# A graph layer with top-p attention: queries split by other engines in the opening, late keys and their load moved between the steps

## The chip, the cores and the metric

The kernel runs on one core of one Trainium2 chip. The core has five engines with a queue each: TensorE (PE: matmuls and transposes into PSUM; its weight loads are shown apart as PEld), VectorE (DVE), ScalarE (ACT), GpSimd (POOL) and SyncE (SP), which here only issues DMAs. Each engine works off its own queue in order and waits on semaphores for the others. The metric is the device time of one execution in microseconds (us).

## The reference

3327 nodes with 256 features each, a sparse weighted adjacency (about 0.12% of the entries beside the diagonal), two steps. Cut to what matters:

```python
def top_p_attention(X, W1, W2, W3):
    q = X @ W1.T @ W2.T                      # 64 wide
    k = X @ W3.T
    probs = softmax(q @ k.T)
    # per row: sort, keep the largest entries until their sum reaches 0.9, drop the rest
    A = probs * mask
    return A / A.sum(-1)

h = relu(layernorm(x))
R = adj + I;  R = R / R.sum(-1)
Xf = Xa = h;  Z = 0
for n in range(2):
    A  = top_p_attention(Xa, W1, W2, W3)
    Xf = R @ Xf
    Xa = A @ Xa
    Z  = Z + Xf @ U1[n].T + Xa @ U2[n].T
out = x + layernorm(h + Z) * ln_g + ln_b
```

## The kernel before, in words

Rows are handled in NT = 26 tiles of 128 nodes (P = 128); NP = 3328 columns. Two fp32r halves stand for one fp32 number: a value is rounded (high part) and the rest is kept beside it (low part), so that the logits of a tile are two accumulating matmuls per 512 columns. `keys` (128 x 3328) holds the rounded keys in rows 0 to 63 and the rest in rows 64 to 127. The queries lie split in DRAM as `qx` and whole as `asks` on the chip.

**Opening** (L1060 to L1130). A loop over q treats the tiles in 13 pairs k, as a pipeline written in program text: at q = k the statistics of the layer norm (DVE, POOL: `rn`), at q = k + 1 the Relu (ACT) and PE's transposes into `pt`, at q = k + 2 ACT's copy of them (`xw` in the rows) and the products for keys and queries into the PSUM tile `pk`, at q = k + 3 the copies out of it, at q = k + 4 the split of keys and queries and the stores. `pk` and `pt` share two PSUM buffers. At q = k + 3 ACT writes the rounded keys (L1064, `keys`), DVE the raw keys and queries (L1065, `kq`) and, for pairs that enter the moments, a copy `krs` (L1067). At q = k + 4 DVE subtracts the rounded keys from the raw ones (L1104), POOL casts the queries (L1106, `qs`) and subtracts (L1107), and SP stores `kq` into `asks` (two DMAs, L1109) and `qs` into `qx` (L1110). `kq` and `qs` are drawn from one set of four buffers with the tag s1. For the first three tiles `qs` is also sent on as the queries `qT` of the first logits (`fetch`, L550).

In the same loop, at q = 5 to 14, `listed` (L862) reduces the adjacency of one tile, in halves of 832 KB, to lists of its nonzero blocks: SP loads a half one ahead (L869, into `wide` and `e`), DVE reduces it (L879, `fm`). After the loop come the moments of the keys, three tiles' `project` (L562 to L577, DVE, ACT and POOL) and the first tile's guess. The order of the opening is not written out: the planner of the tile framework orders each queue by the program's order and by what its cost model holds to be ready, and it makes an instruction wait for a buffer until its last reader is done. Products for the diffusion (`products`, L1027: PE L1039, copies L1045, stores L1046 and L1047) start in the opening and run on in the first tiles.

**Steps** (L1176 to L1280). From `begin` on, each engine's order is the order of the text (L1283 to L1287; SP's until step 1 starts). For step 0 and 1 and i = -1 to 27, seven parts k = 0 to 6 run what the strings of PLAN, BEGIN, OPEN and LAST name by letters: w is a tile's logits and exponentials (`weights`, four chunks of 832 columns, L634 and L636), d its settling on DVE (L756 to L794), s the sparse diffusion (L955, L1157, and the store L1160 of `vx`), e the end of a tile of step 0 (`first_end`, L963: PE L968, ACT L969 and L971, POOL L972, the store `sx`, and then `prep`).

`prep` (L497) makes the keys and queries of step 1 from a finished tile of step 0. For tiles below SPOOLED = 22 the columns of `keys` are still in use, so the rounded and the low part go to `kx` in DRAM; for tiles 22 to 25 the keys are written in place (ACT L514, DVE L522), and POOL splits the queries (L523, L524). The stores are collected in a list and issued on SP by `stored` (L553): at part k = 4 of each i, and from i = 23 on also at the end of each i. At i = 24 SP issues the load of the 22 spooled tiles from `kx` into `keys` in three DMAs (L1233): tiles 0 to 6, 7 to 12 and 13 to 21. They wait for the stores that they read. The first three chunks of step 1's first tiles run from i = 24 on, the fourth in step 1.

Of the kernel before, what the change touches and what calls it, by code (L numbers as in the profile page):

```python
# [9 lines left out]
F32 = mybir.dt.float32  # L10
F32R = mybir.dt.float32r
# [4 lines left out]
ALU = mybir.AluOpType  # L16
# [3 lines left out]
P = 128  # L20
# [3 lines left out]
NT = (N + P - 1) // P  # L24
# [301 lines left out]
HALF = NT // 2  # L326
# [21 lines left out]
def guess_graph_layer(ctx, tc, x, adj, w1t, w2t, w3t, u1t, u2t, ln_g, ln_b, out, flag):  # L348
# [148 lines left out]
    def prep(xT, t):  # L497
        pk = ps_t.tile([P, 4, P], F32, tag="pt", name="pk")
        for c in range(ND):
            PE.matmul(pk[:, 0, :], wk[:, c, :], xT[:, c, :], start=c == 0, stop=c == ND - 1)  # L500
        if t in COUNTED:
            for c in range(ND):
                PE.matmul(pk[:, 1, :DA], xT[:, c, :], wk[:, c, :DA], start=c == 0, stop=c == ND - 1)
        kr = krs[:, t // 2 % 2, :]
        if t in COUNTED:
            S.copy(kr[:, :DA], pk[:, 1, :DA])
        kq = tpool.tile([P, P], F32, tag="kq", name="kq", bufs=2)
        hi = tpool.tile([P, P], F32R, tag="hi", name="hi", bufs=2)
        lo = tpool.tile([P, P], F32R, tag="lo", name="lo", bufs=2)
        at = slice(t * P, (t + 1) * P)  # L510
        if t < SPOOLED:
            S.copy(hi, pk[:, 0, :])
        else:
            S.copy(keys[low, at], pk[low, 0, :])  # L514
        S.copy(kq, pk[:, 0, :])
        yield
        if t < SPOOLED:
            G.tensor_tensor(lo, kq, hi.bitcast(F32), ALU.subtract)
            stores.append((kx[low, at], hi[low]))
            stores.append((kx[high, at], lo[low]))  # L520
        else:
            V.tensor_tensor(keys[high, at], kq[low], keys[low, at].bitcast(F32), ALU.subtract)  # L522
            G.tensor_copy(hi[high], kq[high])  # L523
            G.tensor_tensor(lo[high], kq[high], hi[high].bitcast(F32), ALU.subtract)  # L524
        stores.append((qx[high, at], hi[high]))
        stores.append((qx[low, at], lo[high]))
        stores.append((query_of(t), kq[high]))
        if t not in COUNTED:
            return
        pg = ps_t.tile([P, 4, P], F32, tag="pt", name="pg")  # L530
        PE.matmul(pg[:DA, 0, : DA + 1], kr[:, :DA], kr, start=True, stop=True)
        gt = small.tile([DA, DA + 1], F32, tag="gt", name="gt", bufs=2)
        S.copy(gt, pg[:DA, 0, : DA + 1])
        G.tensor_tensor(gsum, gsum, gt, ALU.add)
# [525 lines left out]
    for q in range(HALF + 5):  # L1060
        if 0 <= q - 3 < HALF:
            k, pk = q - 3, made.pop(q - 3)
            raw[k] = kq = row.tile([P, 2, P], F32, tag="s1", name="kq", bufs=4)
            S.copy(keys[low, 2 * k * P : (2 * k + 2) * P], pk[low, :2, :].rearrange("p t r -> p (t r)"))  # L1064
            V.tensor_copy(kq, pk[:, :2, :])  # L1065
            if 2 * k in COUNTED:
                V.tensor_copy(krs[:, k % 2, :DA], pk[:, 2, :DA])  # L1067
        if q < HALF:
            mv = small.tile([P, 2, 2], F32, tag="mv2", name="mv2", bufs=4)
            rn = small.tile([P, 2, 2], F32, tag="rn2", name="rn2", bufs=3)  # L1070
            for h in range(2):
                st = small.tile([P, 6], F32, tag="bn", name="st")
                V.bn_stats(st, x0[:, 2 * q + h, :])
                V.bn_aggr(mv[:, h, :], st)
            G.tensor_scalar(rn[:, 0, :], mv[:, :, 1], LN_EPS, None, ALU.add)
            G.tensor_tensor(rn[:, 0, :], rn[:, 0, :], half[:, 0::3], ALU.pow)
            G.tensor_tensor(rn[:, 1, :], mv[:, :, 0], rn[:, 0, :], ALU.mult)
            G.tensor_scalar(rn[:, 1, :], rn[:, 1, :], -1.0, None, ALU.mult)
            scaled[q] = rn
        if 5 <= q < 15:  # L1080
            run(lister, 1)
        if 0 <= q - 2 < HALF:
            k, pt = q - 2, turned.pop(q - 2)
            S.copy(hT[:, 2 * k : 2 * k + 2].rearrange("p t c r -> p (t c) r"), pt)
            pk = ps_t.tile([P, 4, P], F32, tag="pt", name="pk")
            for c in range(ND):
                PE.matmul(pk[:, :2, :], wk[:, c, :], hT[:, 2 * k : 2 * k + 2, c, :], start=c == 0, stop=c == ND - 1)
            if 2 * k in COUNTED:
                for c in range(ND):
                    PE.matmul(pk[:, 2, :DA], hT[:, 2 * k, c, :], wk[:, c, :DA], start=c == 0, stop=c == ND - 1)  # L1090
            made[k] = pk
        if 0 <= q - 1 < HALF:
            k, rn = q - 1, scaled.pop(q - 1)
            pt = ps_t.tile([P, 4, P], F32, tag="pt", name="pt")
            for h in range(2):
                t = 2 * k + h
                S.activation(x0[:, t, :], x0[:, t, :], AF.Relu, bias=rn[:, 1, h : h + 1], scale=rn[:, 0, h : h + 1])
                for c in range(ND):
                    PE.transpose(pt[:, 2 * h + c, :], x0[:, t, c * P : (c + 1) * P], ident)
            turned[k] = pt  # L1100
        if 0 <= q - 4 < HALF:
            k, kq = q - 4, raw.pop(q - 4)
            at = keys[:, 2 * k * P : (2 * k + 2) * P]
            V.tensor_tensor(at[high], kq[low].rearrange("p t r -> p (t r)"), at[low].bitcast(F32), ALU.subtract)  # L1104
            qs = row.tile([P, 2, P], F32R, tag="s1", name="qs", bufs=4)
            G.tensor_copy(qs[high], kq[high])  # L1106
            G.tensor_tensor(qs[low], kq[high], qs[high].bitcast(F32), ALU.subtract)  # L1107
            for h in range(2):
                nc.sync.dma_start(query_of(2 * k + h), kq[high, h, :])  # L1109
            nc.sync.dma_start(qx[:, 2 * k * P : (2 * k + 2) * P], qs.bitcast(F32).rearrange("p t r -> p (t r)"))  # L1110
            for h in range(2):
                if 2 * k + h < 3:
                    fetch(0, 2 * k + h, qs[:, h, :])
        if 0 <= q - 4 < HALF and 2 * (q - 4) in COUNTED:
            k = q - 4
            kr = krs[:, k % 2, :]
            PE.matmul(pgram[:DA, : DA + 1], kr[:, :DA], kr, start=2 * k == COUNTED[0], stop=2 * k == COUNTED[-1])
        if q == 6:
            run(begun[0], 1)
        if q in (8, 11, 14):  # L1120
            run(begun[0], 1)
        if q in (9, 12):
            run(begun[q // 3 - 2], 1)
        if q == 5:
            for n in range(2):
                nc.sync.dma_start(u1[:, :, n], u1t[n].rearrange("(c p) e -> p c e", p=P))
# [68 lines left out]
    for step in range(2):  # L1195
        sums = Sums(step, live, xw if step else x0, AHEAD[step])

        for i in range(-1, NT + 2):
# [30 lines left out]

                work["w"] = itertools.islice(begun[i - NT + 2], CUT - 1)  # L1230
            if step == 0 and i == NT - 2:
                for a, b in ((0, 7), (7, 13), (13, SPOOLED)):
                    nc.sync.dma_start(keys[:, a * P : b * P].bitcast(F32), kx[:, a * P : b * P])  # L1233
            if step == 0 and i >= NT - 3 and i < NT:
                fetch(1, i - NT + 3)
# [3 lines left out]
            if step == 0 and i == 0:  # L1239
                work["w"] = begun[2]  # L1240
            for k in range(PARTS):
                if step == 0 and k == 4:
                    stored()
                g = PARTS * (i - 1) + k - LATE[step]
                summing = valid(g // PARTS)
                if step and valid((g + AHEAD[1]) // PARTS):
                    sums.turn(g + (k == 2), min(i, NT - 1))
                for c in ({**OPEN, **LAST} if step else BEGIN).get(i, PLAN[step])[k]:
                    at = len(trace)
                    next(work[c], None)  # L1250
                    if c == "g" and not step and len(trace) > at:
                        gate = next(n for n in reversed(trace[:at]) if n.engine == S.engine)
                        issue = next(n for n in trace[at:] if n.engine == G.engine)
                        tc.add_manual_dep(issue, gate.name, BEHIND, reason="one by one")
                if summing and not step:
                    sums.turn(g, min(i, NT - 1))
                for n in BLOCKS[step].get(k, (0,)) if summing else ():
                    ended = sums.sum(g + n)
                    if ended and step == 0:
                        live["r", ended[0]] = ended[1]  # L1260
                    elif ended:
                        work["f"] = finish(ended[0], live.pop(("f", ended[0])), *ended[1])
# [5 lines left out]
                next(fetching)  # L1268
            for c in ("lcnwqsepb" if i > -1 else "cnwqsepb") if step else "ocmwqseph" + "b" * (i > 0):
                run(work[c])  # L1270
            if step == 0 and i >= NT - 3:
                stored()
            if step == 0 and i == NT:
                moments(1, gsum)
# [53 lines left out]
```

## Time and profile before

| | |
|---|---|
| median of 3 runs | 1392.1 us (1389.31 to 1393.02) |
| the profiled execution | 1390.78 us, its span 1389.0 us |
| instructions | 22547 |
| PE busy | 1239.2 us, 89% |
| PEld busy | 1030.9 us, 74% |
| DVE busy | 1196.2 us, 86% |
| ACT busy | 1068.8 us, 77% |
| POOL busy | 1036.2 us, 75% |
| opening and first tiles | to about 190 us |
| steady part of step 0 | about 190 to 620 us |
| between the steps | about 620 to 830 us |

A row of the view in order of time gives start, duration, engine, line, operation, output <- input and shapes; what stands in brackets is how long the engine was idle before it, and what ended that. SPq is SP's queue: its rows are the issue of a DMA, not the transfer. In the list of groups the number after the bar is busy us and mean ns, and after the second bar the idle time before the group with its releasers. A row of waits reads: engine, line, what it waited for, total us, times, longest us.

### The profile page before, as it was taken

The page shows a single profiled execution, that of the slowest core. Times are in us where ns is not written, and L with a number is a line of the kernel's source. Part 1 is how long each engine was busy: PE and PEld are TensorE (multiplying, and loading weights), DVE is VectorE, ACT ScalarE, POOL GpSimd, SP SyncE. Part 2 cuts the span into 40 slices and gives each one's busy share as a digit, 9 for nine tenths or more (in the row PEclk, how much of TensorE's full clock was granted, in tenths as well). Part 3 has the DMA queues.
Part 4 walks back from the last instruction along what each step waited for, and adds up shares of the span by engine and source line. Part 5 has one row for each costly group of instructions (what it writes and reads, how often), then busy time and mean ns, then how long its engine had stood idle before and what let it go on. Part 6 is the DMA issues. An engine that isn't in the chain of part 4 may idle for free.

```text
span 1389.0 us, 22547 instructions
## 1 busy us (share of the span) xinstructions
PE 1239.2 (89%) x6340; PEld 1030.9 (74%) x6340; DVE 1196.2 (86%) x3652; ACT 1068.8 (77%) x2226; POOL 1036.2 (75%) x1460
## 2 busy tenths in 40 slices
PE   5759899999999999999879849999999999999985
PEld 4524688888887888888768647878878887787874
DVE  5748789999999999999874489899998999999994
ACT  5365687878788887878754589898998989999851
POOL 6322588888888888887865477888888888888832
PEclk9989999999999999999999979999999999999998
DMA  5844555555555555555544222313223132231200
GB/s 182 268 155 130 148 147 157 151 163 154 166 147 171 145 165 149 152 165 150 151 125 125 71 64 59 99 54 99 71 79 94 56 97 70 81 95 50 89 23 22
DMA packets 123191, 164.59 MB, mean 118 GB/s; under 512 B 21137, under 2 KB 89232, under 8 KB 123056
## 3 DMA queue, kind: packets, MB, share of 16 engines
q1 hardware_dynamic: 105520, 120.14, 27.9%
q0 software_dynamic: 16640, 42.69, 12.0%
q8 instruction: 53, 0.87, 0.3%
q14 instruction: 82, 0.67, 0.2%
q10 hardware_dynamic: 896, 0.21, 0.1%
HBM read 128.74 MB, written 32.12 MB: 116 GB/s over the span
## 4 chain that ended last, share of the span: by engine, by line
DVE 51%; PE 15%; ACT 14%; POOL 9%; issue 4%; DMA 3%; SPq 1%; DVEq 0%; POOLq 0%; ACTq 0%
DVE cand L761 9%; DVE w L756 8%; ACT ja L660 8%; DVE e L790 8%; PE pa L849 6%; DVE fm L879 5%; DVE cand L770 4%; DVE bb L768 4%; PE pl L634 2%; PE pz L1039 2%; ACT e L636 2%; PE pt L836 2%; POOL xg L947 2%; POOL g L739 2%; PE pr L955 1%
## 5 line engine op out<-in xcount | busy, mean ns | idle before, releaser
L660 ACT ACTIVATE ja<-e,g 128x3328 uint8<-128x3328 f32 x106 | 325.9, 3074 | 0.1
L849 PE MATMUL pa<-x,eT 128*128 128x256 f32 x1352 | 322.0, 379 | 0.0
L849 PE MATMUL pa<-xw,eT 128*128 128x256 f32 x1352 | 318.1, 380 | 3.0 <-DVE s L979 3.0
L849 PEld LDWEIGHTS pa<-xw,eT 128*128 128x128 f32 x1352 | 251.3, 190 | 36.1 <-DVE s L979 4.9
L849 PEld LDWEIGHTS pa<-x,eT 128*128 128x128 f32 x1352 | 242.8, 190 | 25.5
L761 DVE MAX8 cand<-w 128x8 f32<-128x168 f32 (+1 forms) x1040 | 253.3, 317 | 0.0
L838 ACT COPY eT<-pt 128x512 f32<-128x512 f32 (+1 forms) x364 | 199.4, 555 | 61.1 <-PE pt L836 61.0
L947 POOL DMA_INDIRECT xg<-bx,index x130 | 189.7, 1460 | 51.5 <-issue 21.9
L634 PE MATMUL pl<-keys,qT 128*128 128x512 f32 (+1 forms) x832 | 200.4, 377 | 26.3 <-ACT e L636 13.7
L836 PE MATMUL pt<-ident,e 128*128 128x128 f32 x1144 | 176.5, 277 | 48.5 <-DVE e L790 34.5
L926 POOL DMA_INDIRECT ac<-in_adj,index x130 | 163.3, 1256 | 67.6 <-ACT e L1045 18.8
L836 PEld LDWEIGHTS pt<-ident,e 128*128 128x128 f32 x1144 | 141.5, 145 | 89.2 <-issue 50.9
L636 ACT ACTIVATE e<-pl 128x832 f32<-128x832 f32 (+1 forms) x176 | 150.6, 862 | 44.9 <-PE pl L634 41.9
L634 PEld LDWEIGHTS pl<-keys,qT 128*128 128x128 f32 x832 | 145.2, 195 | 52.0 <-ACT e L636 15.9
L947 POOL DMA_INDIRECT xg<-vx,index x130 | 150.5, 1158 | 34.1 <-issue 32.8
L756 DVE SCALAR_TENSOR_TENSOR w<-e,g 128x3328 f32<-128x3328 f32 x44 | 164.3, 3734 | 4.2 <-ACT g L741 4.1
L790 DVE SCALAR_TENSOR_TENSOR e<-e,rec 128x3328 f32<-128x3328 f32 x40 | 148.3, 3708 | 0.6
L955 PE MATMUL pr<-xg,ac 128*128 128x257 f32 (+1 forms) x520 | 139.1, 392 | 10.1 <-DVE s L1157 8.4
L955 PEld LDWEIGHTS pr<-xg,ac 128*128 128x128 f32 x520 | 95.4, 195 | 21.8 <-DVE s L1157 8.8
L768 DVE MAX8 bb<-cand 128x8 f32<-128x160 f32 x286 | 92.6, 324 | 6.4
L879 DVE TENSOR_REDUCE fm<-at 128x4 f32<-128x512 f32 (+1 forms) x133 | 84.3, 634 | 5.5 <-DMA at<-in_adj 5.5
L703 POOL TENSOR_SCALAR g<-g,law 128x1 f32<-128x1 f32 x23 | 65.6, 2850 | 10.9 <-ACT g L702 10.1
(260 smaller groups left out, 2018.4 us busy)
## 6 DMA issues: line engine op xcount, KB each, us to landing
at<-in_adj SPq DMA_DIRECT2D x114, 256.0 KB
cx<-ac SPq DMA_DIRECT2D x26, 384.0 KB
ac<-cx SPq DMA_DIRECT2D x26, 384.0 KB
wide<-in_adj SPq DMA_DIRECT2D x8, 832.0 KB
qT<-qx SPq DMA_DIRECT2D x196, 32.0 KB
e<-in_adj SPq DMA_DIRECT2D x6, 832.0 KB
own<-bx SPq DMA_DIRECT2D x26, 128.5 KB
x<-in_x SPq DMA_DIRECT2D x13, 256.0 KB
```

Source lines behind the costliest of these rows:

```text
L634: PE.matmul(pl[:, a:b], qT[:, k, :], keys[:, c + a : c + b], start=k == 0, stop=k == 1)
L636: S.activation(e[:, c : c + w], pl[:, :w], AF.Exp, accum_out=za[:, n : n + 1])
L660: S.activation(ja, e, f, bias=guess, scale=sign, accum_out=total)
L756: V.scalar_tensor_tensor(w, e, col(16), e, ALU.is_lt, ALU.mult, accum_out=d2)
L761: V.max(cand[:, 8 * s : 8 * s + 8], w[:, s * SEG : min(NP, (s + 1) * SEG)])
L790: V.scalar_tensor_tensor(e, e, at(1), e, ALU.is_ge, ALU.mult, accum_out=ra)
L836: PE.transpose(pt[:, j, :], e[:, (j0 + j) * P : (j0 + j + 1) * P], ident)
L838: S.copy(eT[:, :w, :], pt[:, :w, :])
L849: PE.matmul(self.pa, eT[:, c - 4 * k, :], self.xa[:, c, :], start=c == 0, stop=c == NT - 1)
L926: G.indirect_dma_start(out=ac[:, k, :], out_offset=None, in_=rows, in_offset=bass.IndirectOffsetOnAxis(ap=index[:, t, k : k + 1], axis=0), ...
L947: G.indirect_dma_start(out=xg[:, k, :w], out_offset=None, in_=rows, in_offset=bass.IndirectOffsetOnAxis(ap=index[:, t, k : k + 1], axis=0))
L955: PE.matmul(pr[:, :w], ac[:, k, :], own if k == KT - 1 else xg[:, k, :w], start=k == 0, stop=k == KT - 1)
```

## The change

Two places. In the opening, ACT copies and casts the queries out of PSUM at q = k + 3 (`qs[high]`), beside its copy of the keys, and DVE subtracts at q = k + 4; POOL has no part in it. `qs` has buffers of its own, those of the tags own and xa (two each, taken in turn), and `kq` keeps the four of s1 alone. The stores of `kq` and `qs` and the sending on to `qT` move from q = k + 4 to q = k + 5.

Between the steps, the low part of the keys of tiles 22 to 24 is subtracted by POOL instead of DVE (tile 25 stays with DVE). The load of the spooled keys is issued in two places: tiles 0 to 12 where all three DMAs were, and tiles 13 to 21 at part k = 2 of the same i, behind the stores of tile 21, which are issued there too (at k = 2 and not at k = 4, and not at the end of the i before). The stores at the end of an i are left at i = 27 only.

```diff
@@ prep
-            V.tensor_tensor(keys[high, at], kq[low], keys[low, at].bitcast(F32), ALU.subtract)
+            (V if t == NT - 1 else G).tensor_tensor(keys[high, at], kq[low], keys[low, at].bitcast(F32), ALU.subtract)
@@ opening, for q in range(HALF + 5)
         if 0 <= q - 3 < HALF:
             k, pk = q - 3, made.pop(q - 3)
-            raw[k] = kq = row.tile([P, 2, P], F32, tag="s1", name="kq", bufs=4)
+            kq = row.tile([P, 2, P], F32, tag="s1", name="kq", bufs=4)
+            qs = row.tile([P, 2, P], F32R, tag=("own", "xa")[k % 2], name="qs", bufs=2)
             S.copy(keys[low, 2 * k * P : (2 * k + 2) * P], pk[low, :2, :].rearrange("p t r -> p (t r)"))
+            S.copy(qs[high], pk[high, :2, :])
             V.tensor_copy(kq, pk[:, :2, :])
+            raw[k] = kq, qs
...
         if 0 <= q - 4 < HALF:
-            k, kq = q - 4, raw.pop(q - 4)
+            k, (kq, qs) = q - 4, raw[q - 4]
             at = keys[:, 2 * k * P : (2 * k + 2) * P]
             V.tensor_tensor(at[high], kq[low].rearrange("p t r -> p (t r)"), at[low].bitcast(F32), ALU.subtract)
-            qs = row.tile([P, 2, P], F32R, tag="s1", name="qs", bufs=4)
-            G.tensor_copy(qs[high], kq[high])
-            G.tensor_tensor(qs[low], kq[high], qs[high].bitcast(F32), ALU.subtract)
+            V.tensor_tensor(qs[low], kq[high], qs[high].bitcast(F32), ALU.subtract)
+        if 0 <= q - 5 < HALF:
+            k, (kq, qs) = q - 5, raw.pop(q - 5)
             for h in range(2):
                 nc.sync.dma_start(query_of(2 * k + h), kq[high, h, :])
             nc.sync.dma_start(qx[:, 2 * k * P : (2 * k + 2) * P], qs.bitcast(F32).rearrange("p t r -> p (t r)"))
...
@@ steps
             if step == 0 and i == NT - 2:
-                for a, b in ((0, 7), (7, 13), (13, SPOOLED)):
+                for a, b in ((0, 7), (7, 13)):
                     nc.sync.dma_start(keys[:, a * P : b * P].bitcast(F32), kx[:, a * P : b * P])
...
             for k in range(PARTS):
-                if step == 0 and k == 4:
+                if step == 0 and k == (2 if i == NT - 2 else 4):
                     stored()
+                    if i == NT - 2:
+                        nc.sync.dma_start(keys[:, 13 * P : SPOOLED * P].bitcast(F32), kx[:, 13 * P : SPOOLED * P])
...
-            if step == 0 and i >= NT - 3:
+            if step == 0 and i == NT + 1:
                 stored()
```

## The prediction

> **What bounds the kernel now.** I read the page first, then a table of stretches, and inside the two stretches that the change touches the groups, the waits and the instructions in order of time. A count before a name in brackets, such as (x57), is a number of instructions.
>
> ```profile
> core 0: us, PE busy (x) PEld busy (x) DVE busy (x) ACT busy (x) POOL busy (x), PEclk, DMA share, GB/s
> 27.14:69.39 42.25, 32.09 (x160) 23.02 (x160) 28.62 (x79) 17.83 (x38) 16.97 (x39) 0.96 0.75 234
> ...
> 190.00:620.00 430.00, 418.02 (x2244) 355.12 (x2244) 412.39 (x1290) 356.56 (x845) 366.10 (x441) 1.00 0.56 157
> ...
> 702.00:778.00 76.00, 67.68 (x342) 55.99 (x340) 37.25 (x123) 30.61 (x77) 42.57 (x59) 0.96 0.40 116
> ```
>
> In the long steady stretch of step 0 PE and DVE are both 96 to 97% busy; the change does not touch it, so whatever is won or lost ahead of it should move it as a whole. The two stretches that are touched have slack: in 42.25 us of the opening the busiest engine works 32.09, and between the steps DVE works 37 of 76.
>
> In the opening the third and the thirteenth copy of raw keys and queries (kq) start at 27.14 and 69.39: ten stages, 4.2 us each. What sets that pace is a loop through a shared buffer. From the instructions in order of time:
>
> ```profile
> 27.14 0.42 DVE L1065 COPY kq<-pk 128x256 f32<-128x256 f32 x1 [1.43 <-ACT keys L1064]
> ...
> 54.76 1.11 SPq L1109 DMA_DIRECT2D asks<-kq  x2
> ...
> 56.50 0.40 POOL L1106 CAST qs<-kq 64x256 fp32r<-64x256 f32 x1 [0.90 <-DMA asks<-kq]
> ...
> 56.98 0.72 POOL L1107 TENSOR_TENSOR qs<-kq,qs 64x256 fp32r<-64x256 f32 x1
> ...
> 57.70 0.41 DVE L1065 COPY kq<-pk 128x256 f32<-128x256 f32 x1
> ...
> 69.39 0.41 DVE L1065 COPY kq<-pk 128x256 f32<-128x256 f32 x1
> ```
>
> kq is copied (53.9 in the stage shown), SP stores it, POOL waits until that store has landed before it may write the split (qs) into a buffer of the same four, and the next kq starts at 57.70, as POOL ends (56.98 + 0.72). The waits, as us in total, times and longest, of POOL and DVE up to 150 us and of SP up to 110 us:
>
> ```profile
> POOL qs L1106 <- DMA asks<-kq: 15.7, 7, 5.4
> ...
> DVE fm L879 <- DMA e<-in_adj: 16.8, 4, 11.5
> ```
>
> ```profile
> SPq L1110 <- POOL qs L1107: 19.7, 10, 4.7
> ```
>
> SP stands 19.7 us behind POOL's split, and the loads of adj, which DVE's list reductions (fm) want, are queued behind it.
>
> Between the steps PE stops once:
>
> ```profile
> 701.84 0.38 PE L490 MATMUL pt<-ident,xa 128*128 128x128 f32 x2
> 709.84 3.14 PE L634 MATMUL pl<-keys,qT 128*128 128x512 f32 x8 [7.62 <-DMA keys<-kx]
> ```
>
> ```profile
> 695.04 0.32 SPq L974 DMA_DIRECT2D sx<-sv  x1
> ...
> 703.20 0.45 SPq L555 DMA_DIRECT2D kx<-lo  x1
> ...
> 705.75 1.49 SPq L1233 DMA_DIRECT2D keys<-kx  x3
> ```
>
> All three loads of the keys stand behind the store of tile 21's low part, which waits for POOL until 703.17.
>
> **The change part by part.** The durations are those of the profiled execution: span 1389.0, time 1390.78. The runs shown have a median of 1392.1, that is 1.3 more. The sum is made against 1390.8 and 1 us is added at the end.
>
> *Opening, loop.* Per stage POOL loses a cast and a subtraction, ACT gains a copy of the form of its keys copy, DVE a subtraction of the form of its keys subtraction. From the groups of 27.14 to 69.39:
>
> ```profile
> L879 DVE TENSOR_REDUCE fm<-e 128x13 f32<-128x1664 f32 x4 | 7.5, 1887 | 5.3 <-DMA e<-in_adj 5.3
> L879 DVE TENSOR_REDUCE fm<-wide 128x13 f32<-128x1664 f32 x4 | 7.5, 1887 | 1.3 <-DMA wide<-in_adj 1.2
> L1104 DVE TENSOR_TENSOR keys<-kq,keys 64x256 fp32r<-64x256 f32 x10 | 4.2, 419 | 0.4
> ...
> L1064 ACT CAST keys<-pk 64x256 fp32r<-64x256 f32 x10 | 3.6, 364 | 11.3 <-PE pk L1090 9.9 <-PE pk L1087 1.2
> ```
>
> The loop through the buffer goes: kq alone has the four buffers of s1, qs takes four others, and kq's stores have two stages before their buffer is wanted again. Next late is DVE or the DMA. DVE: 28.62 busy + 10 x 0.42 = 32.8 us. DMA: 0.75 x 42.25 = 31.7 us of work, if it ran without a hole. So at most 42.25 - 32.8 = 9.4 us are to be had. I take 5: the reductions are uneven (every second stage closes a list), and ACT, PE and DVE hand the tile on to each other, so that 88% busy (32.8 / 37.3) is what I believe and not 100%.
>
> ACT's copy is not free everywhere. In the first stages, before 27 us, ACT's Relu and its copy of the transposed tile follow its keys copy directly:
>
> ```profile
> 22.39 0.37 ACT L1064 CAST keys<-pk 64x256 fp32r<-64x256 f32 x1 [1.93 <-PE pk L1090]
> ...
> 23.24 0.59 ACT L1084 COPY xw<-pt 128x512 f32<-128x512 f32 x1
> ...
> 23.88 2.08 PE L1087 MATMUL pk<-xw,wk 128*128 128x256 f32 x4 [0.68 <-ACT xw L1084]
> ```
>
> PE waits for that copy (0.68), so each of three such stages gets 0.37 longer: 1.1 lost. From 27 on I cost ACT's copies at nothing: ACT works 17.83 of 42.25 there, and PE's next tile does not need the copied one's memory until a stage later; without that cover they cost 10 x 0.37 = 3.7. The stores a stage later cost nothing either: they are the last readers of their buffers, which are wanted two stages on. Net of the loop: **-4**, ends -8.3 (9.4 - 1.1) and +1.1 (nothing won).
>
> *Opening, tail.* POOL does the moments of three tiles before its last two splits, and SP's queue stands:
>
> ```profile
> 80.58 0.43 SPq L869 DMA_DIRECT2D e<-in_adj  x1
> ...
> 85.68 1.76 PE L634 MATMUL pl<-keys,qT 128*128 128x512 f32 x4 [10.96 <-ACT e L636]
> ...
> 87.23 4.40 PE L1039 MATMUL pz<-u,xw 128*128 128x512 f32 x8
> 88.05 1.89 DVE L879 TENSOR_REDUCE fm<-e 128x13 f32<-128x1664 f32 x1 [11.46 <-DMA e<-in_adj]
> ...
> 91.14 1.28 DVE L1045 COPY e<-pz 128x512 f32<-128x512 f32 x2
> ```
>
> With DVE's split SP is past this point at least 4.7 us earlier (its longest wait above), and DVE's 11.46 us of waiting shrink. But DVE's next step, the copies at 91.14, needs PE's products, ended at 87.23 + 4.40 = 91.6, and these stand behind the chunk at 85.68, which waited 10.96 us for an exponential of ACT that the change does not touch. So the tail moves with the loop and I count 0 for it; the other end is -4.7.
>
> *Between the steps.* Two of the three loads no longer stand behind tile 21's store: they follow the sx store of 695.04, and even three took until 709.8 from 705.75, so two land before 700. PE's two chunks of logits at 709.84 read columns 0 to 1663, tiles 0 to 12, which is what they bring. PE goes on at 702.2: 7.6 us. What follows the stop is also slow:
>
> ```profile
> 675.24 1.76 PE L634 MATMUL pl<-keys,qT 128*128 128x512 f32 x8
> ```
>
> ```profile
> 700.00:720.00 20.00, 12.38 (x57) 10.03 (x56) 14.15 (x52) 10.59 (x19) 10.15 (x15) 0.83 0.53 164
> ...
> 740.00:760.00 20.00, 20.00 (x109) 17.02 (x108) 6.44 (x15) 7.99 (x20) 12.39 (x14) 1.00 0.49 134
> ```
>
> Eight matmuls took 3.14 where they take 1.76, at a granted clock of 0.83: 1.4 more, 9.0 together. [...] The row's 1.4 is used.
>
> Where the stall goes:
>
> ```profile
> 714.06 0.35 DVE L905 TENSOR_SCALAR oh<-place,over,lists 128x128 f32<-128x128 f32 x1 [5.20 <-ACT lists L902]
> ...
> 717.00 3.69 DVE L790 SCALAR_TENSOR_TENSOR e<-e,rec 128x3328 f32<-128x3328 f32 x1
> ```
>
> ```profile
> 721.65 1.01 PE L634 MATMUL pl<-keys,qT 128*128 128x512 f32 x4
> ...
> 725.28 0.61 PE L836 MATMUL pt<-ident,e 128*128 128x128 f32 x4
> ```
>
> The third chunk would come at 721.65 - 9.0 = 712.6 and the third load lands by 709.8 as it does now, since its place behind tile 21's store stays. DVE can move by its own wait only, 5.2: its e is done at 717.00 + 3.69 - 5.2 = 715.5, and PE turns it at 725.28 - 9.0 = 716.3. Both fit, the second by 0.8. Afterwards PE is busy 20.00 of 20 us, so what it wins here arrives at the end of the step. I take **-8.5**, ends -9.4 and -5.2.
>
> The moved subtractions (tiles 22 to 24), and the stores of these tiles:
>
> ```profile
> 726.04 0.28 DVE L522 TENSOR_TENSOR keys<-kq,keys 64x128 fp32r<-64x128 f32 x1 [2.17 <-ACT kq L515]
> ```
>
> ```profile
> 734.18 0.46 POOL L524 TENSOR_TENSOR lo<-kq,hi 64x128 fp32r<-64x128 f32 x1
> ```
>
> DVE loses 3 x 0.28 and its waits for kq, but it works 37 of 76 us there, so nothing; POOL gains 3 x 0.46 = 1.4 and works 42.57 of 76. These keys are first read by a first tile's last chunk in step 1, after the last tile's own keys, so POOL's 1.4 are covered; bare they would cost 1.4. The stores leave the ends of tiles for the fifth part of the next; SP then no longer holds vx and own behind them. Nobody reads them before step 1: 0.
>
> Sum: 1390.8 - 4 - 8.5 = 1378.3, and 1379 against the runs.
>
> **The rivals.** *Only the step change counts.* kq stands behind both ACT copies of the same PSUM tile: in the row at 27.14 it started when ACT's keys copy ended. If that lies in every stage's path, ten stages get 3.7 longer, the cold ones 1.1, and of 5 won nothing is left: 1390.8 - 8.5 = 1382.3, about 1383. Against it: the tile has a spare beside it, and DVE, not PE, is next late. [...]
>
> *The opening gives all.* DVE runs without a hole and the tail follows SP: 1390.8 - 8.3 - 4.7 - 8.5 = 1369.3, 1370. For it: DVE's waits are nearly all for the loop that goes. Against: PE's wait for ACT in the tail.
>
> *The stall only moves.* Tile 21's low part on POOL (703.17) or the e of DVE is late once more, the third chunk waits, and the step change gives a quarter, -2; with the opening 1390.8 - 4 - 2 = 1384.8, about 1386. For it: the 0.8 us of room. Against: the third load has 2.8.
>
> *Slower.* The opening's order is the planner's, not written out. With the buffer loop gone it may put a reduction fm in DVE's queue ahead of kq before its load has landed; then DVE holds kq, PE and the next load. From the chain of waits:
>
> ```profile
> 93.70 5.17 DMA wide<-in_adj
> ```
>
> Such a stage takes 5.17 + 1.89 (fm) + 1.26 (kq and two subtractions) = 8.3 and not 4.2. For the four reductions from e, which wait now, that is 16.4: 1390.8 + 16.4 - 8.5 = 1398.7, about 1400. It ends slower than before from 8.5 / 8 = 1.1 us more for each of eight reductions. Against it: these waits are 5.3 + 1.3 us now, in a queue blocked by POOL.
>
> **How the numbers follow.** Forecast 0.52 (own range 1372 to 1384), only the step 0.18, opening gives all 0.12, the stall only moves 0.11, slower 0.07. The likeliest is 1379. The range 1370 to 1388 leaves out the slower case and the outer tails. A measurement can tell 0.3%, 4.2 us: faster means below 1387.9. Faster: 0.52 + 0.15 + 0.12 + 0.05 = 0.84; same: 0.03 + 0.06 + 0.01 = 0.10; slower 0.06.
>
> **What would show it.** The opening: POOL's wait for asks gone, the thirteenth kq near 65, DVE above 85% busy between third and thirteenth; right in the tail if PE's wait for ACT stays near 11 us while DVE's 11.5 shrinks. Between the steps: no wait of PE for keys over 1 us, L634's eight at 1.8 and not 3.1, and the stretch from the stopped chunk to the last product some 8 us shorter. I am wrong if the stage stays at 4.2, if DVE's waits for adj grow, if PE's 7.6 us reappear as a wait for DVE's e or the third load, or if the steady stretch gets longer.

## The result, and the profile after

The changed kernel takes 1380.25 us (median of 4, 1379.45 to 1380.84) against 1392.56 us of the kernel before (median of 4, 1389.31 to 1394.04): a ratio of 0.9914, 95% interval 0.9896 to 0.9933. That is 1.2 us from the predicted 1379. But the profile after shows that the sum came out so close by luck: the opening, counted at 4 us, gave nothing that shows, and what came between the steps and behind them is 2 us more than the 8.5 counted there.

To place the gain I read when DVE starts the first pass over a tile (L756, the settling pass), here for tile 0, tile 23, and the first tile of step 1, by the instructions in order of time. Before:

```profile
104.02 3.68 DVE L756 SCALAR_TENSOR_TENSOR w<-e,g 128x3328 f32<-128x3328 f32 x1
...
668.82 4.23 DVE L756 SCALAR_TENSOR_TENSOR w<-e,g 128x3328 f32<-128x3328 f32 x1
...
800.92 3.69 DVE L756 SCALAR_TENSOR_TENSOR w<-e,g 128x3328 f32<-128x3328 f32 x1 [1.97 <-ACT g L741]
```

After:

```profile
106.62 3.69 DVE L756 SCALAR_TENSOR_TENSOR w<-e,g 128x3328 f32<-128x3328 f32 x1
...
668.51 4.25 DVE L756 SCALAR_TENSOR_TENSOR w<-e,g 128x3328 f32<-128x3328 f32 x1
...
791.11 3.69 DVE L756 SCALAR_TENSOR_TENSOR w<-e,g 128x3328 f32<-128x3328 f32 x1 [1.98 <-ACT g L741]
```

Tile 0 is 2.6 us later than before, tile 23 is 0.3 us earlier, the first tile of step 1 is 9.8 us earlier. The spans (1389.0 and 1378.2) differ by 10.8: 0.3 up to tile 23, 9.5 between the steps, 1.0 in the rest of step 1.

**The opening's loop got longer.** The third and thirteenth copy `kq` start at 26.37 and 78.52: 5.2 us a stage, against 4.2 before. The row of the table of stretches (columns as in the prediction):

```profile
26.37:78.52 52.15, 40.12 (x156) 29.15 (x157) 34.23 (x97) 22.28 (x50) 7.57 (x22) 0.71 0.62 203
```

DVE is 66% busy there (34.23 of 52.15), not the 85% that the prediction asked for, and PE's granted clock is 0.71 where it was 0.96. The waits from 20 to 110 us (total us, times, longest us) name what is late:

```profile
DVE kq L1067 <- ACT qs L1066: 15.2, 10, 2.7
...
PEld pt L1102 <- ACT qs L1066: 10.2, 6, 1.8
```

POOL's wait for the store of `asks` is gone, as predicted. In its place DVE's copy `kq` waits for ACT's new copy `qs`, ten times, nine of them between the third and the thirteenth copy. PE's next transposes wait for it too, since `pt` takes the PSUM buffer that it leaves. One stage in order of time:

```profile
52.28 2.07 PE L1090 MATMUL pk<-xw,wk 128*128 128x256 f32 x4 [0.27 <-ACT xw L1087]
...
54.15 0.95 PE L1093 MATMUL pk<-wk,xw 128*128 128x64 f32 x4
...
55.14 0.37 ACT L1065 CAST keys<-pk 64x256 fp32r<-64x256 f32 x1 [2.91 <-PE pk L1093]
55.53 0.37 ACT L1066 CAST qs<-pk 64x256 fp32r<-64x256 f32 x1
55.93 0.42 DVE L1067 COPY kq<-pk 128x256 f32<-128x256 f32 x1 [2.69 <-ACT qs L1066]
...
56.73 1.09 PE L1102 MATMUL pt<-ident,x 128*128 128x128 f32 x4 [1.62 <-DVE fm L884]
...
57.85 0.59 ACT L1087 COPY xw<-pt 128x512 f32<-128x512 f32 x1 [1.96 <-PE pt L1102]
```

Here every step waits for the one above it, and each of ACT, DVE and PE shows an idle time in brackets. What a row doesn't print is which pair a copy belongs to. The order of ACT's rows gives it. For the first five pairs `qs` stands right behind `keys` of the same pair. Then come these, where ACT's other rows are left out:

```profile
35.51 0.35 ACT L1065 CAST keys<-pk 64x256 fp32r<-64x256 f32 x1
...
37.95 0.37 ACT L1065 CAST keys<-pk 64x256 fp32r<-64x256 f32 x1
...
38.34 0.37 ACT L1066 CAST qs<-pk 64x256 fp32r<-64x256 f32 x1
```

The sixth pair's `keys` (35.51) are followed by the seventh's (37.95), and the `qs` behind those is the sixth pair's. So it goes on to the end, where a thirteenth `qs` stands alone at 78.12: from the sixth pair on the planner put `qs` of pair k *behind* `keys` of pair k + 1. The starts of `kq` show the same break: the third to the fifth follow each other by 2.7 and 3.6 us (26.37, 29.10, 32.70), the sixth to the thirteenth by 5.2 to 6.3. The `qs` at 55.53 is of the pair before the `keys` at 55.14. So the loop is: products of pair k + 1, ACT's keys of k + 1, ACT's queries of k, DVE's `kq` of k, PE's transposes into the buffer that this frees, ACT's `xw`, products of pair k + 2.

**The tail got shorter.** From the start of the thirteenth `kq` to tile 0's settling pass it was 104.02 - 69.39 = 34.6 us and is 106.62 - 78.52 = 28.1, that is 6.5 us less. SP's load of adj, DVE's reduction of it and PE's chunk that waits for ACT, after:

```profile
82.42 0.43 SPq L869 DMA_DIRECT2D e<-in_adj  x1
...
90.47 1.89 DVE L879 TENSOR_REDUCE fm<-e 128x13 f32<-128x1664 f32 x1 [5.61 <-DMA e<-in_adj]
...
94.69 1.75 PE L634 MATMUL pl<-keys,qT 128*128 128x512 f32 x4 [10.76 <-ACT e L636]
```

Before, this load was issued at 80.58, which is 11.2 us after the thirteenth `kq`; now it is 3.9 us after it. From that issue to tile 0's pass it is 23.4 us before and 24.2 after.

**Between the steps** PE no longer stops. After:

```profile
695.56 1.98 SPq L1236 DMA_DIRECT2D keys<-kx  x2
...
702.95 0.38 PE L490 MATMUL pt<-ident,xa 128*128 128x128 f32 x2
703.09 1.77 PE L634 MATMUL pl<-keys,qT 128*128 128x512 f32 x8
...
706.58 0.46 SPq L1248 DMA_DIRECT2D keys<-kx  x1
```

The two chunks follow the transpose without a wait, and their eight matmuls take 1.77 us instead of 3.14. The third load goes out at 706.58, no earlier than before, and no wait for it shows.

### The profile page after: what moved, and what is told of

The parts are those of the page before. It is cut to its first block, busy times and chain, and to the rows that moved or that the text cites. A ratio compares the mean times of both kernels' runs of the same rounds, so it can differ in the third digit from the quotient of the medians.

```text
span 1378.2 us, 22545 instructions
## 1 busy us (share of the span) xinstructions
PE 1240.7 (90%) x6340; PEld 1031.5 (75%) x6340; DVE 1200.3 (87%) x3662; ACT 1071.7 (78%) x2239; POOL 1028.8 (75%) x1437
## 3 DMA queue, kind: packets, MB, share of 16 engines
q1 hardware_dynamic: 105520, 120.14, 27.8%
## 4 chain that ended last, share of the span: by engine, by line
PE 49%; DVE 24%; ACT 15%; POOL 5%; issue 3%; DMA 1%; SPq 0%; another core or an unknown queue 0%; DVEq 0%; POOLq 0%; ACTq 0%
PE pa L849 20%; ACT ja L660 8%; PE pl L634 7%; PE pt L836 6%; PE pr L955 5%; DVE cand L761 5%; DVE w L756 4%; PE pz L968 3%; PE pz L1039 3%; DVE e L790 3%; DVE cand L770 2%; DVE bb L768 2%; ACT e L636 2%; POOL g L739 2%; PE pk L1090 1%
## 5 line engine op out<-in xcount | busy, mean ns | idle before, releaser
L947 POOL DMA_INDIRECT xg<-bx,index x130 | 192.5, 1481 | 50.2 <-issue 26.8
L926 POOL DMA_INDIRECT ac<-in_adj,index x130 | 159.8, 1229 | 54.4 <-issue 26.4
L756 DVE SCALAR_TENSOR_TENSOR w<-e,g 128x3328 f32<-128x3328 f32 x44 | 164.0, 3728 | 4.4 <-ACT g L741 4.3
L660 ACT ACTIVATE ja<-x,g 128x3328 uint8<-128x3328 f32 x24 | 73.7, 3070 | 0.0
```

Source lines behind the costliest of these rows:

```text
L660: S.activation(ja, e, f, bias=guess, scale=sign, accum_out=total)
L756: V.scalar_tensor_tensor(w, e, col(16), e, ALU.is_lt, ALU.mult, accum_out=d2)
L926: G.indirect_dma_start(out=ac[:, k, :], out_offset=None, in_=rows, in_offset=bass.IndirectOffsetOnAxis(ap=index[:, t, k : k + 1], axis=0), ...
L947: G.indirect_dma_start(out=xg[:, k, :w], out_offset=None, in_=rows, in_offset=bass.IndirectOffsetOnAxis(ap=index[:, t, k : k + 1], axis=0))
```

## The experiments

The theory formed from the two traces: the change between the steps is worth some 10 us, the opening nothing, because its loop, freed from the shared buffer, is caught by ACT's copy of the queries out of PSUM, which stands too late in ACT's queue. The rival is the prediction's own split, 4 and 8.5.

All kernels in one table. "Ten stages" is third to thirteenth `kq`; "tail" thirteenth `kq` to tile 0's settling pass; "between" tile 23's pass to the first of step 1; all three in us and from the profiled execution. The kernel before had medians of 1390.3 to 1391.3 in the sessions of e1 to e11. Intervals are 95%. How far one profiled execution can be trusted shows where kernels have the same code: the four with the opening of before (before, e1, e7, e8) have ten stages of 42.25 to 44.77 and tails of 34.6 to 35.3, and the nine with the whole change between the steps have 122.2 to 123.8 there.

| kernel | us | ratio to before | ten stages | tail | between |
|---|---|---|---|---|---|
| before | 1392.56 | | 42.25 | 34.6 | 132.1 |
| after | 1380.25 | 0.9914 (0.9896 to 0.9933) | 52.15 | 28.1 | 122.6 |
| e1 steps only | 1380.55 | 0.9918 (0.9886 to 0.9951) | 43.44 | 35.2 | 122.6 |
| e2 opening only | 1389.93 | 0.9994 (0.9975 to 1.0014) | 52.03 | 28.5 | 132.0 |
| e3 queries cast from `kq` | 1370.06 | 0.9863 (0.9821 to 0.9905) | 38.78 | 28.7 | 123.8 |
| e4 `kq` ahead of ACT | 1376.24 | 0.9871 (0.9827 to 0.9914) | 40.10 | 29.0 | 123.7 |
| e5 queries ahead of keys | 1373.30 | 0.9884 (0.9858 to 0.9910) | 41.51 | 27.8 | 122.6 |
| e6 POOL's split, own buffers | 1366.91 | 0.9841 (0.9814 to 0.9868) | 35.68 | 28.8 | 122.3 |
| e7 load only | 1379.12 | 0.9915 (0.9896 to 0.9935) | 44.77 | 34.9 | 123.5 |
| e8 late keys on POOL only | 1390.04 | 0.9993 (0.9976 to 1.0010) | 43.62 | 35.3 | 131.2 |
| e9 as e6, stores not later | 1369.72 | 0.9842 (0.9820 to 0.9863) | 37.13 | 29.0 | 122.2 |
| e10 after, PE kept busy | 1376.47 | 0.9895 (0.9875 to 0.9915) | 45.00 | 27.2 | 123.0 |
| e11 as e6, `kq` ahead of ACT | 1372.46 | 0.9871 (0.9846 to 0.9895) | 40.92 | 27.2 | 122.9 |

**The two halves, e1 and e2.** The kernel before with only the hunks between the steps, and with only those of the opening.

> The kernel before with the edits between the steps alone. The prediction's terms: -8.5, so 1384. Theory formed from the two traces (the change between the steps is worth about 10 and the opening nothing): the first settling pass of step 1 starts 9 to 11 us earlier than before, and the time is 1381 to 1383. If the two places help each other (the opening's shift lets a load between the steps land earlier), less than both: 1386 or more.

> The kernel before with the edits of the opening alone. The prediction's term: -4, so 1388.5, and the tenfold stage of the loop at 37 us. Theory: the loop takes 52 us for ten stages as in the changed kernel (42.25 before), since the copy of raw keys and queries waits for ACT's copy of the same tile's queries, which stands in ACT's queue behind the next tile's keys; the tail gives it back, because SP no longer stands behind POOL; the time is 1391 to 1394, the same as before.

e1 takes 1380.55, the whole gain of the change; e2 1389.93 with the ratio 0.9994, no difference. (Both are a little under what the theory expected, 1381 to 1383 and 1391 to 1394.) In e2 the stage is as long as in the changed kernel and the tail as short. So the gain is that of the steps, and the prediction's 4 us for the opening did not come: e2's interval reaches to 3.5 us of gain, and 4 lie just outside it.

**What makes the loop, e3, e4, e5.** e3 takes ACT's second read out of PSUM:

```diff
-            S.copy(qs[high], pk[high, :2, :])
             V.tensor_copy(kq, pk[:, :2, :])
+            S.copy(qs[high], kq[high])
```

> The changed kernel, with ACT's cast of the queries taken from the copy kq in the SBUF, after DVE's copy, and no more from the PSUM tile pk. Nothing else moves. Theory (ACT's copy in the PSUM tile's chain paces the loop): no wait of kq for qs, the next transposes do not wait for it, ten stages take 36 to 42 us and the granted clock of PE is over 0.9 there; the time is 1370 to 1376 if the tail keeps what it won, and 1379 to 1381 if the tail takes it back. Rival (the pace of 5.2 us is DVE's extra subtraction, or the loads of adj, which no longer find SP late): ten stages stay at 50 to 53 us, the time at 1380.

e4 lets DVE copy first:

```diff
+            V.tensor_copy(kq, pk[:, :2, :])
             S.copy(keys[low, 2 * k * P : (2 * k + 2) * P], pk[low, :2, :].rearrange("p t r -> p (t r)"))
             S.copy(qs[high], pk[high, :2, :])
-            V.tensor_copy(kq, pk[:, :2, :])
```

> The changed kernel, with DVE's copy of raw keys and queries ahead of ACT's two copies of the same PSUM tile in the program's order, so that ACT waits for DVE and not DVE for ACT. Theory (DVE's copy behind ACT's queries, which stand behind the next tile's keys, makes the loop): ten stages take 36 to 43 us; the PSUM tile still comes free only after ACT's copies, so a little more than with the queries cast from the SBUF; the time is 1371 to 1377 or, if the tail takes it back, 1379 to 1381. Rival (any copy of the queries out of PSUM holds the tile): ten stages at 48 us or more, the time at 1380.

e5 only exchanges ACT's two lines; both still read PSUM ahead of `kq`, but in the built queue `qs` of a pair now stands directly before `keys` of the same pair:

```diff
+            S.copy(qs[high], pk[high, :2, :])
             S.copy(keys[low, 2 * k * P : (2 * k + 2) * P], pk[low, :2, :].rearrange("p t r -> p (t r)"))
-            S.copy(qs[high], pk[high, :2, :])
```

> The changed kernel with two lines exchanged: ACT's copy of the queries out of the PSUM tile stands ahead of its copy of the keys, and in its queue no copy of queries stands behind the next tile's keys any more. DVE's copy still waits for both, and both still read PSUM. Theory (it is the place in ACT's queue, a stage late, that makes the loop): ten stages 39 to 44 us, PE's clock over 0.9, the time 1371 to 1377. Rival (any two reads of the PSUM tile by ACT ahead of DVE's copy make the loop, whatever their order): ten stages 48 us or more, the time 1379 to 1381.

The rows of the third to the thirteenth `kq`, of e3:

```profile
25.59:64.37 38.78, 30.48 (x152) 21.91 (x151) 33.47 (x92) 20.95 (x46) 6.27 (x18) 0.93 0.84 273
```

and of e5:

```profile
25.25:66.76 41.51, 32.29 (x156) 23.00 (x155) 33.97 (x98) 21.13 (x48) 6.74 (x21) 0.92 0.75 256
```

All three end the long loop. DVE's work is the same as in the changed kernel (33.5 to 34.0, against 34.23), so it was not DVE's added subtraction. e5 is the sharpest of the three: exchanging two lines takes 52.15 to 41.51 and the time to 1373.30. (e4 changes two things, since in it `qs` stands right behind `keys` of its own pair again.) The place in ACT's queue is what made the loop. Whether the two reads out of PSUM as such cost something more is open: from e5 to e3 it is another 2.7 us in ten stages, hardly more than the 2.5 by which kernels with the same opening differ. In e3 DVE is 86% busy (33.47 of 38.78). e4's time spreads over 1368.16 to 1378.50, and cannot be told from e3 or e5.

**Is the split on ACT and DVE needed at all? e6, e9, e11.** e6 has POOL's cast and subtraction as before, in the changed kernel's own buffers:

```diff
-            S.copy(qs[high], pk[high, :2, :])
...
-            V.tensor_tensor(qs[low], kq[high], qs[high].bitcast(F32), ALU.subtract)
+            G.tensor_copy(qs[high], kq[high])
+            G.tensor_tensor(qs[low], kq[high], qs[high].bitcast(F32), ALU.subtract)
```

> The changed kernel with POOL's cast and subtraction of the queries back as before, while the split has buffers of its own and the stores stay a stage later. What it tells: how much of the gain with a free loop is the shared buffer and how much is POOL and SP. Theory: the loop through the buffer is gone, ten stages take 38 to 42 us; but the last splits stand behind POOL's moments again, so that the time from the last copy of raw keys and queries to the first settling pass is 33 to 35 us (34.6 before, 28 to 29 in the changed kernel): 1376 to 1380. Rival (the split's engine does not matter, the shared buffer is everything): that time falls to 28 or 29 as well, and the kernel reaches 1369 to 1373.

The stretch in e6:

```profile
27.08:62.76 35.68, 29.86 (x160) 21.59 (x160) 29.74 (x81) 17.53 (x38) 17.36 (x39) 1.00 0.87 290
```

1366.91 us, the best kernel here: 35.68 us for ten stages at a granted clock of 1.00. The rival of that expectation holds: the tail falls to 28.8 although POOL splits. I had laid the tail to POOL's split standing in front of SP; it is the shared buffer that made POOL's split late. In order of time, e6:

```profile
67.76 0.43 SPq L869 DMA_DIRECT2D e<-in_adj  x1
...
91.58 3.69 DVE L756 SCALAR_TENSOR_TENSOR w<-e,g 128x3328 f32<-128x3328 f32 x1
```

The load goes out 5.0 us after the thirteenth `kq` (62.76), and the pass follows it by 23.8 us: the third kernel in which the tail is some 24 us from this load's issue. In all thirteen kernels of the table this distance is 23.0 to 24.3 us, while from PE's chunk that waits 10 to 11 us for ACT to the pass it is 8.5 to 18.3.

e9 moves the stores back to q = k + 4:

```diff
-        if 0 <= q - 5 < HALF:
-            k, (kq, qs) = q - 5, raw.pop(q - 5)
```

> As the kernel with POOL's split in buffers of its own, but with the stores back at q = k + 4, right behind the split. It tells the buffers from the stores' place. If SP's place behind POOL's split held the loads of adj (SP stood 19.7 us there before): SP waits for POOL 15 to 20 us again, the time from the last copy of raw keys and queries to the first settling pass is 33 to 35 us, and the kernel takes 1371 to 1376. If the shared buffer alone was the loss: 28 to 30 us there and 1366 to 1369, as with the later stores.

1369.72 and a tail of 29.0: SP's waits for POOL stay away even so. In e1, which still has the shared buffer, SP waits between 20 and 110 us:

```profile
SPq L1110 <- POOL qs L1107: 20.7, 10, 5.2
```

In e9 no row of more than 1.2 us names POOL. So it is the buffer, and the stores' later place is worth nothing that these runs can tell (the intervals of e6 and e9 overlap).

e11 puts DVE's copy first in e6:

> As the kernel with POOL's split in buffers of its own and the later stores, with DVE's copy of raw keys and queries ahead of ACT's copy of the keys, so that ACT waits for DVE. In that kernel DVE waited 4.6 us for ACT's keys in four stages. If that is in the path: ten stages 33 to 35 us (35.7) and 1363 to 1366. If the loads of adj (DMA share 0.87 there) or the queue orders set the pace: 35 to 37 us and 1366 to 1369; and if ACT's wait for DVE delays the turned tile: 38 us or more and 1369 to 1373.

The last of its cases came: 40.92 us and 1372.46. What helped where `kq` was behind two copies of ACT makes the loop longer where it was behind one: ACT's keys (10.3 us in all) and PE's next transposes (7.4) now wait for DVE. The intervals of the two ratios, e6's and e11's, still overlap.

**How much of the loop is the clock, e10.** The changed kernel, with two products more per stage that nobody reads:

```diff
             turned[k] = pt
+        if 0 <= q - 2 < HALF:
+            fill = ps_r.tile([P, 2 * D], F32, tag="pr", name="fill")
+            for c in range(ND):
+                PE.matmul(fill[:, : 2 * P], wk[:, c, :], hT[:, 2 * (q - 2) : 2 * (q - 2) + 2, c, :], start=c == 0, stop=c == ND - 1)
```

> The changed kernel with two more products (128x256, from the turned tile already there, into PSUM that nobody reads) on PE in each stage of the opening, in the time in which PE waits. Nothing else moves. If the low granted clock (0.67 to 0.71 in ten stages) is a part of the loss of the loop: the clock rises above 0.85, pk's four matmuls take under 1.5 us instead of 2.07, ten stages take 42 to 48 us in spite of the added work, and the time is 1371 to 1377. If the clock is only a mark of the waiting: each stage takes the added 0.5 to 1.1 us more, ten stages 55 to 62 us, and the time is 1383 to 1390.

Seven stretches of 5 us of the changed kernel, inside the loop:

```profile
42.00:47.00 5.00, 3.42 (x17) 2.63 (x16) 2.29 (x12) 1.53 (x4) 0.43 (x1) 0.82 1.00 349
47.00:52.00 5.00, 3.51 (x14) 2.63 (x12) 3.97 (x8) 1.83 (x5) 0.00 (x0) 0.52 1.01 360
52.00:57.00 5.00, 3.11 (x11) 2.56 (x11) 2.26 (x6) 0.97 (x3) 0.00 (x0) 0.50 0.88 281
57.00:62.00 5.00, 4.42 (x16) 3.29 (x14) 3.08 (x9) 1.11 (x3) 0.43 (x1) 0.62 0.39 109
62.00:67.00 5.00, 4.05 (x16) 3.18 (x16) 3.29 (x5) 1.75 (x4) 0.00 (x0) 0.73 0.46 174
67.00:72.00 5.00, 3.11 (x11) 2.18 (x10) 3.89 (x13) 1.32 (x3) 0.43 (x1) 0.50 0.14 39
72.00:77.00 5.00, 3.56 (x8) 1.70 (x7) 3.73 (x10) 0.73 (x2) 0.00 (x0) 0.50 0.14 39
```

and of e10, with a stage in order of time below:

```profile
47.00:52.00 5.00, 4.02 (x23) 3.14 (x23) 4.21 (x6) 1.75 (x5) 0.00 (x0) 1.00 1.01 339
52.00:57.00 5.00, 4.17 (x22) 2.81 (x21) 4.32 (x14) 1.62 (x4) 0.42 (x1) 1.00 0.98 339
```

```profile
49.98 1.13 PE L1090 MATMUL pk<-xw,wk 128*128 128x256 f32 x4 [0.41 <-ACT xw L1087]
50.95 0.56 PE L1093 MATMUL pk<-wk,xw 128*128 128x64 f32 x4
51.34 1.08 PE L1107 MATMUL fill<-xw,wk 128*128 128x256 f32 x4
```

With 1.08 us more work in each stage the ten stages take 45.00 us instead of 52.15, at a clock of 1.00; `pk`'s four matmuls take 1.13 and not 2.07. ACT's queue is the same as in the changed kernel (`qs` still behind the next `keys`). So some 7 us of the loop's loss go with the clock, which is 1.00 in these ten stages, where products fill PE's short waits, against 0.71; the waits are the queue's. The profiled execution of e10 is its fastest (1371.38; the other three take 1376 to 1377), so the ten stages may be a little flattered; the ratio, 0.9895, holds all four.

**The halves of the step change, e7 and e8.** e7 has the load in two parts and the stores' place, e8 the one hunk with POOL's subtraction.

> The kernel before with the keys' load in two parts and the stores' new place alone; DVE keeps the late keys. The prediction's term: PE's 7.6 us and the slow matmuls go, 1.4; 1381 to 1384 by it. Theory from the trace of the changed kernel: the stall goes and DVE's moment sums of the last tiles still wait behind the key subtractions, so 8 to 9.5 us of the 10: 1381 to 1383. Rival (without POOL's subtraction DVE is late with e and PE waits there): half of it, 1385 or more.

> The kernel before with the late keys' subtraction on POOL alone. The prediction's term: nothing, 1390 to 1392, and PE's stop of 7.6 us stays. Theory from the trace of the changed kernel: 0.5 to 1.5 us, because DVE's moment sums and PE's products behind them no longer stand behind tile 24's keys (DVE's wait for ACT there), so 1389 to 1391. Rival (it costs POOL's covered time): slower by 1 to 1.5.

e7 takes 1379.12, less than the 1381 to 1383 that were expected and no more than e1: by the whole time the load alone gives all that the step change gives. By the "between" column it gives 132.1 - 123.5 = 8.6 us of the 9.5 of e1, and e8 gives 0.9; but 123.5 lies among the 122.2 to 123.8 of the kernels with the whole step change. So one profiled execution does not tell 8.6 from 9.5, nor 0.9 from nothing, and e8's time cannot be told from before. The waits of e7 between 690 and 800 us show what e8 takes away:

```profile
DVE keys L522 <- ACT kq L515: 21.2, 3, 15.0
```

and those of e8 that the stop stays:

```profile
PE pl L634 <- DMA keys<-kx: 7.3, 1, 7.3
```

DVE stood up to 15 us at a subtraction of late keys, and the moment sums of the next step's scale (`qm`, L539) stood behind it: in the changed kernel they are at 745.8, before at 769.6. That this wins time is not shown: PE's products from `qm` (L562) start without idle time in both (761.93 and 770.47), and in the changed kernel DVE waits 16.3 us for ACT at `mq` (L570) instead.

## Why the prediction was right, and where it was wrong

- **The total**: 1378.3 by the sum, 1379.95 in the profiled execution. Right, but by luck: the opening's term of 4 was too high by nearly all of it (0.3 up to tile 23, and no difference in e2), and about half of that was made up by 1.0 more than 8.5 up to tile 0 of step 1 and 1.0 more in the rest of step 1. The sum of the rival *Only the step change counts*, 1382.3, is 2.4 off, the forecast's 1.6: the total alone does not choose between them, e1 and e2 do, and they speak for the rival.
- **Opening, the loop through the buffer**: the mechanism was right. POOL's wait for `asks` went, and e9, where of the opening only the buffers differ from before, takes 37.13 us for ten stages instead of 42.25.
- **Opening, "From 27 on I cost ACT's copies at nothing"**: this is the step that failed. The cover named there, that PE's next tile does not need the copied one's memory until a stage later, was no cover, since the copy itself came a stage later: `kq` and PE's transposes waited for it (15.2 and 10.2 us). The rival *Only the step change counts* had the right place, `kq` behind both ACT copies, and the right outcome for the opening; but its price of 3.7 us (the copy's own length, ten times) was less than half of the 9.9 us lost (7.4 against the slowest kernel with the opening of before). I priced a wait by the duration of the instruction, where the queue put another pair's products in front of it; and PE's granted clock was 0.71 in these ten stages, against 0.92 in e5 and 1.00 in e10. Without that copy in PSUM's path, the prediction's loop comes: 37.3 was worked out, e3 has 38.78, DVE 86% busy against 88%.
- **Opening, tail**: counted 0, ends -4.7 and 0, measured -6.5. The argument that DVE's copies wait for PE's products, which wait 11 us for ACT, took a chain that runs beside for one that holds: DVE's copies at 91.14 show no idle time, so they did not wait for PE's products. PE's wait stays, at 10.8 us, and DVE's for adj shrinks to 5.6, which the prediction had named as the sign of being right here; the tail moves all the same. It goes with the issue of adj's load, some 24 us ahead of the pass in every kernel. From tile 0 to tile 23 the changed kernel then takes 2.9 us less than before and e2 3.8 less, but e7, with the opening of before, takes 2.7 less too, and e1 takes as long as before: that is what kernels differ by, and no gain of the opening can be read from it.
- **Stores a stage later**: 0, and e9 against e6 cannot tell it from 0.
- **Between the steps, the stop and the slow matmuls**: 7.6 + 1.4 = 9.0, taken 8.5; the load alone gave 8.6 by e7's trace, with the moved subtraction 9.5 in e1. The mechanism was right: PE's stop is gone, the eight matmuls take 1.77 us, and DVE's `e` and the third load fitted, as worked out. For the end of 9.4 that stands beside the 8.5 no run shows a source; the runs showed 8.6 and 9.5 in its place.
- **Moved subtraction**: 0 taken, for an engine with slack, and no run tells it from 0: e8's trace shows 0.9, within what traces differ by, and its ratio is 0.9993 (0.9976 to 1.0010). Slack alone was no reason, since DVE stood *in front of* the moment sums at a wait for ACT of 15 us; but PE's products from these sums did not wait for them.
- **The stall only moves** and **Slower**: neither came. No reduction was put ahead of `kq` at a cost; what the planner did place badly was on ACT, where I had not looked.

## What to carry to other kernels

When a copy is added to a tile in PSUM that another engine reads too, ask where the planner will put it in its queue, not only how long it takes: here a late place made the later reader `kq` wait 15.2 us and the next user of that buffer 10.2, in all. Before work is moved off an engine because that engine is waited for, find what the engine itself waits for; here a buffer of its own for the split, with the split left on POOL, gave 1366.91 against 1380.25. Read each term of a sum at its own place in the trace after: a total that is right within 1.2 us hid a term of 4 that was nothing.

## What the runs showed of the hardware that was not expected

PE's granted clock fell without a long pause. Between 27 and 79 us of the changed kernel the longest idle time of PE is 1.62 us, in the row of transposes above (56.73); still the clock is 0.50 to 0.52 in stretches in which PE is busy 3.11 to 3.56 of 5 us. With more work in the same gaps, at 4.02 and 4.17 of 5 us, it is 1.00 (e10). What sets it, and at which share of busy time it falls, these rows do not show: in e10's stretch from 37 to 42 us PE's records add up to 2.93 of 5 us, and the clock is 1.00 there. Nor is busy time the same measure at every clock: `pk`'s four matmuls take 2.07 us in the stretch at 0.50 (52 to 57 us) and 1.13 us at 1.00 (e10), so that 4.42 of 5 us stands beside a clock of 0.62.
